# Three named double banks for scores and other products in a two-layer attention kernel

## The chip, the cores and the metric

The kernel runs on one core of one Trainium2 chip. The metric is the device time of one launch in microseconds (us), the median of three runs: 4044.44 us before the change (4041.61 to 4047.32). TensorE is called PE here, VectorE DVE, ScalarE ACT, GpSimd POOL and SyncE SP, as in the profile. [...]

## The reference

The input x is 4 images of 32 x 32 tokens with 768 channels, float32. Two layers run one after the other, each with a residual:

```
x = x + L0(gn(x))      # q, k, v = h @ W + b;  softmax(q k / 8 + bias_h + bias_w) v;  @ Wp + bp
x = x + L1(gn(x))      # the same, but each of q, k, v goes through a depthwise 3x3
                       # convolution and a layer norm over each head's 64 channels,
                       # and q is added to the head's output before the projection
```

`gn` is a group norm over 32 groups. There are 12 heads of 64 channels. The position bias of a query and a key is the query times a table that depends on the distance of their rows, plus the same for their columns. All is in float32.

## The kernel before, in words

The eight stages are images in pairs: images 0 and 1 in layer 0, the same two in layer 1, then images 2 and 3. A stage has six items, one for each pair of heads (two heads fill 128 partitions), so there are 48 items. An item's attention (`attend`) has 16 steps: two halves of the queries (512 columns), and in each two groups of four key tiles of 128 keys.

In a group, four chunks of scores come first. A chunk is a product of k and q for both heads (L669), to which a product of a one-hot matrix with the position bias is added (L671); ACT then takes its exponential (L676) out of two PSUM banks, one for each head. Behind the four chunks stands other work of PE, then the weighted sum of v for the four key tiles (L690, "av"), then other work again. DVE adds the exponentials up for the denominators (L682, L684).

The other work belongs to the next item: q, k and v products and what follows them. A table of steps (`plan`, `at`, `events`) says at which step each piece is issued; steps 0, 1, 4, 5, 8, 9, 12 and 13 fall behind scores and the others behind av. The order on PE, DVE, ACT and POOL is exactly the order of issue in the program (a manual schedule), so an instruction that waits holds up all that was issued later on its engine. Waits are set by the framework from which tile an instruction reads and writes. The pieces are:

- `plain` and `plain_v`, for the first two items: a product of 24 or 96 matmul records, and its evacuation by ACT (L410, L411, L419, L400).
- `sevens`, in the other items of layer 0: q and k of an item, or v of two items, come together out of seven products of quarters. The first call makes m4 into one bank, m3 into another, adds m2 to the first and m5 to the second; the second call makes m1 and m7, and adds m6 to m1's bank. ACT copies m4 out (L335), DVE adds (L330, L361, L375), ACT evacuates (L410, L419, L373).
- `padded`, in layer 1: a product, copied by ACT with its bias into a padded image in two parts (L442). `taps` is the convolution on DVE (L457, L459). `centre` takes the mean off by a product (ln_c), ACT squares it (L472) and copies it (L473). `squares` and `norm` finish the layer norm, `back` transposes with PE (ln_t) and ACT evacuates.
- `positions`: the position bias, 64 small matmuls into one bank (rel), copied by ACT in two parts (L522, L523); `split` divides it into two addends and sends them by POOL's DMA queue.
- `sums` and `result`: the denominators (z, L639), ACT's copy, Ln and Exp (L646 to L649), DVE's Newton step and the product with the weighted sum (L654 to L661). They are in a list `rest`, from which `more()` takes one entry at each place behind scores and behind av.
- `project`: the output product (proj), to which DVE adds bias and residual (L723). For the first image a product of weights and v bias (pbias, L713) is added to the bias first, in both layers.
- `group_norm` (two tiny products) and `mix_tokens` (sums of token quarters, L234) for the next stage.

Of PSUM's eight banks, scores have four (`ps_s`, two tiles of two banks, in turn), av has one, and all other products take one of three single banks in turn (`ps_m`, handed out by `bank`).

```
ps_s = pool("ps_s", 2, space=PSUM)
ps_av = pool("ps_av", 1, space=PSUM)
ps_m = pool("ps_m", 3, space=PSUM)
```

Of the kernel before, what the change touches and what calls it, by code (L numbers as in the profile page):

```python
# [9 lines left out]
F32 = mybir.dt.float32  # L10
# [7 lines left out]
P = 128  # L18
# [3 lines left out]
C = 768  # L22
# [23 lines left out]
def two_layers(ctx: ExitStack, tc: tile.TileContext, keep, x_in, wqkv, wproj, rels, windows, vrow, small, const, onehot, picks, out):  # L46
# [25 lines left out]
    work = pool("work", 2)  # L72
    one = pool("one", 1)
    stat = pool("stat", 3)
    ps_s = pool("ps_s", 2, space=PSUM)
    ps_av = pool("ps_av", 1, space=PSUM)
    ps_m = pool("ps_m", 3, space=PSUM)

    def bank(name):
        return ps_m.tile([P, 512], F32, tag="bank", name=name)  # L80

    def halves(ps, a, b, start=True, stop=True, **kw):

# [153 lines left out]
    def group_norm(stage):  # L237

        xn = xns[stage]
        st = stat.tile([P, NC * 2, 6], F32, tag="bn", name="bn", bufs=1)  # L240
        for n in range(NC):
            for h in range(2):
                nc.vector.bn_stats(st[:, 2 * n + h, :], xn[:, n, h * HALF : (h + 1) * HALF])
            if n in (1, 3):
                yield
        mv = stat.tile([P, 2], F32, tag="mv", name="mv")
        nc.vector.bn_aggr(mv, st.rearrange("p a b -> p (a b)"))
        yield
        yield
        group = cst[:, GROUP : GROUP + P]  # L250
        ps = bank("gn_mean")
        nc.tensor.matmul(ps[:, 0:1], group, mv[:, 0:1], start=True, stop=True)
        mean = stat.tile([P, 1], F32, tag="gmean", name="gmean")
        nc.vector.tensor_copy(mean, ps[:, 0:1])
        d = stat.tile([P, 1], F32, tag="gd", name="gd")
        nc.vector.tensor_sub(d, mv[:, 0:1], mean)
        nc.vector.scalar_tensor_tensor(d, d, d, mv[:, 1:2], ALU.mult, ALU.add)
        yield
        yield
        ps = bank("gn_var")  # L260
        nc.tensor.matmul(ps[:, 0:1], group, d, start=True, stop=True)
        v = stat.tile([P, 1], F32, tag="gv", name="gv")
        nc.vector.tensor_scalar(v, ps[:, 0:1], EPS, None, ALU.add)
        yield
        r = rsqrt(v, 1, "gn")
        yield
        for n in range(NC):
            nc.vector.tensor_scalar(xn[:, n, :], xn[:, n, :], mean, r, ALU.subtract, ALU.mult)  # L268
            if n % 2:
                yield  # L270
# [7 lines left out]
    sk = fixed.tile([P, NSMALL], F32, tag="sk", name="sk")  # L278
    nc.vector.tensor_scalar(sk, sm, SCALE, None, ALU.mult)

    pbias = fixed.tile([P, 2, NC], F32, tag="pbias", name="pbias")

    ones = fixed.tile([P, T], F32R, tag="ones", name="ones")
    plain = one.tile([P, T], F32, tag="whole", name="plain")
# [8 lines left out]
    class Pair:  # L293
# [15 lines left out]
        def sevens(self, s, second):  # L309

            xn = xns[self.b, self.layer]
            x11, x12, x21, x22 = (xn[:, n : n + 3, h : h + HALF] for n in (0, 3) for h in (0, HALF))

            def m(ps, at, x, more=False):

                w = weights[self.i, s, at // 2][:, 3 * (at % 2) : 3 * (at % 2) + 3, :]  # L320
                for t in range(4 if s else 1):
                    for n in range(3):
                        flags = dict(start=not (t or n or more), stop=n == 2, skip_group_check=True)
                        if s:
                            tokens = slice(t * P, (t + 1) * P)
                            halves(ps[:, tokens], x[:, n, tokens], w[:, n, :], **flags)
                        else:
                            halves(ps, w[:, n, :], x[:, n, :], **flags)

            add = lambda to, x, y, op=ALU.add: nc.vector.tensor_tensor(to, x, y, op)  # L330
            u, w = terms
            if not second:
                self.banks = b1, b2 = bank("m4m2"), bank("m3m5")
                m(b1, 0, x21)
                nc.scalar.copy(u, b1)  # L335
                m(b2, 1, x12)
                used((self.i, s, 0))
                add(u, u, b2)
                m(b1, 2, x11, more=True)
                add(w, u, b1, ALU.subtract)  # L340
                self.put(s, 1, 0, b1)
                m(b2, 3, x22, more=True)
                used((self.i, s, 1))
                add(u, u, b2, ALU.subtract)
                self.put(s, 0, 1, b2)
            else:
                b3, b4 = bank("m1m6"), bank("m7")
                m(b3, 4, quarters[0])
                add(u, u, b3)
                m(b4, 5, quarters[2])  # L350
                used((self.i, s, 2))
                self.put(s, 0, 0, b4, u)
                m(b3, 6, quarters[1], more=True)
                used((self.i, s, 3))
                self.put(s, 1, 1, b3, w)
# [258 lines left out]
    def attend(pair, os):  # L614
# [12 lines left out]
        for c in range(T // QC):  # L627
# [6 lines left out]

            def sums(weighed, acc, c=c):

                z = bank("z")
                for j in range(2):
                    nc.tensor.matmul(  # L639
                        z[j * D : (j + 1) * D, :], cst[:, ONES : ONES + D], acc[:, j, :],  # L640
                        start=True, stop=True,
                    )
                at = 2 * (pair.i * (T // QC) + c)
                t = work.tile([P, QC], F32, tag="t", name="t", bufs=1)
                inv = work.tile([P, QC], F32, tag="inv", name="inv", bufs=1)
                nc.scalar.activation(t, z, AF.Copy, accum_out=seen[:, at : at + 1])  # L646

                nc.scalar.activation(inv, t, AF.Ln, bias=tiny)
                nc.scalar.activation(inv, inv, AF.Exp, scale=-1.0, accum_out=seen[:, at + 1 : at + 2])  # L649
                return weighed, t, inv  # L650

            def result(weighed, t, inv, cols=cols):

                nc.vector.scalar_tensor_tensor(t, t, -1.0, inv, ALU.mult, ALU.mult)  # L654
                nc.vector.scalar_tensor_tensor(inv, t, 2.0, inv, ALU.add, ALU.mult)

                if pair.layer:
                    nc.vector.tensor_tensor(inv, weighed, inv, ALU.mult)
                    nc.vector.scalar_tensor_tensor(q[:, cols], inv, col(LN + 4), q[:, cols], ALU.mult, ALU.add)
                else:  # L660
                    nc.vector.tensor_tensor(q[:, cols], weighed, inv, ALU.mult)  # L661

            for g in range(0, NKT, 4):
                es = []
                for kt in range(g, g + 4):
                    keys = slice(kt * P, (kt + 1) * P)
                    ps = ps_s.tile([P, 2, QC], F32, tag="s", name="s")
                    for j, rows in enumerate(heads):
                        nc.tensor.matmul(ps[:, j, :], k[rows, keys], q[rows, cols], start=True, stop=False)  # L669
                    for j, rows in enumerate(heads):  # L670
                        nc.tensor.matmul(  # L671
                            ps[:, j, :], ones[rows, keys], bias[c][rows, kt // 2, :],
                            start=False, stop=True,
                        )
                    e = work.tile([P, 2, QC], F32, tag="e", name="e", bufs=4)
                    nc.scalar.activation(e, ps, AF.Exp)  # L676
                    es.append(e)
                more()
                if g == 0:
                    av = ps_av.tile([P, QC], F32, tag="av", name="av")  # L680
# [6 lines left out]
                for t, e in enumerate(es):  # L687
                    kt = g + t
                    for j in range(2):
                        nc.tensor.matmul(  # L690
                            av[j * D : (j + 1) * D, :], pair.vt[:, kt, j * D : (j + 1) * D], e[:, j, :],
                            start=(kt == 0), stop=(kt == NKT - 1),
                        )
                more()
                if g + 4 == NKT:
                    rest.extend((sums, result))
                    found = (copy(av), acc)
                yield
                yield
# [1 line left out]
    def project(stage, os):  # L701
# [3 lines left out]
        for m in range(NC):  # L705
            w = wp.tile([P, NC, P], F32, tag="wproj", name="wproj_t")
            nc.sync.dma_start(w, wproj[layer, :, :, m, :].rearrange("h p q -> p h q"))
            bias = col(BIAS[layer] + 18 + m)
            if b == 0:
                ps = bank("pbias")  # L710
                for n in range(NC):
                    v_bias = col(LN + 5) if layer else col(BIAS[0] + 12 + n)
                    nc.tensor.matmul(ps[:, 0:1], w[:, n, :], v_bias, start=(n == 0), stop=(n == NC - 1))  # L713
                nc.vector.tensor_tensor(pbias[:, layer, m : m + 1], ps[:, 0:1], bias, ALU.add)
            bias = pbias[:, layer, m : m + 1]
            for h in range(2):
                cols = slice(h * HALF, (h + 1) * HALF)
                x = wp.tile([P, HALF], F32, tag="x", name="x")
# [16 lines left out]
    for k in range(1, len(stages)):  # L735
# [5 lines left out]
        if stages[k][1] == 0:  # L741
            mix = mix_tokens(stages[k])
            for r in range(5):
                at(first + 5 * n_steps + r - (0 if stages[k - 1][1] else 8), lambda mix=mix: next(mix, None))
        elif stages[k - 1][1] == 0:
            at(first + 4 * n_steps + 6, lambda: [nc.gpsimd.memset(pad, 0.0) for pad in pads])
    mix = mix_tokens(stages[0])
# [29 lines left out]
    def check():  # L777
# [2 lines left out]
        nc.vector.tensor_reduce(total, seen, AX.X, ALU.add)  # L780
        good = stat.tile([P, 1], F32, tag="good", name="good")
        nc.vector.tensor_scalar(good, total, LIMIT, None, ALU.is_lt)
        ps = bank("good")
        nc.tensor.matmul(ps[:1, :1], cst[:, ONES : ONES + 1], good, start=True, stop=True)
        bad = keep.tile([1, 1], mybir.dt.int32, tag="bad", name="bad")
        nc.vector.tensor_scalar(bad, ps[:1, :1], -1.0, 1.0 * P, ALU.mult, ALU.add)
# [297 lines left out]
```

## Time and profile before

| | before |
|---|---|
| median of 3 runs | 4044.44 us |
| profiled execution, its own time | 4040.44 us |
| its span, first to last instruction | 4038.7 us |
| mean granted TensorE clock | 0.996 |
| PE busy, share of the span | 3945.2 us, 98% |
| DVE busy | 2494.3 us, 62% |
| ACT busy | 1812.1 us, 45% |
| POOL busy | 409.8 us, 10% |

All times of the sections below come from this one execution, so sums are made against its 4040.44 us. A row of the groups reads: line, engine, operation, tile written and tiles read, shape, count, then busy us and mean ns of one, then the idle time of the engine just ahead of them and what ended most of it. In a timeline the first number is the start in us from the span's start and the second the length; rows that follow each other on an engine are merged. A wait's row has the us in total, the times, and the longest. "PEld" is PE loading weights, which overlaps with its products.

### The profile page before, as it was taken

The page shows a single profiled execution, that of the slowest core. Times are in us where ns is not written, and L with a number is a line of the kernel's source. Part 1 is how long each engine was busy: PE and PEld are TensorE (multiplying, and loading weights), DVE is VectorE, ACT ScalarE, POOL GpSimd, SP SyncE. Part 2 cuts the span into 40 slices and gives each one's busy share as a digit, 9 for nine tenths or more (in the row PEclk, how much of TensorE's full clock was granted, in tenths as well). Part 3 has the DMA queues.
Part 4 walks back from the last instruction along what each step waited for, and adds up shares of the span by engine and source line. Part 5 has one row for each costly group of instructions (what it writes and reads, how often), then busy time and mean ns, then how long its engine had stood idle before and what let it go on. Part 6 is the DMA issues. An engine that isn't in the chain of part 4 may idle for free.

```text
span 4038.7 us, 79929 instructions
## 1 busy us (share of the span) xinstructions
PE 3945.2 (98%) x35098; PEld 1720.3 (43%) x35098; DVE 2494.3 (62%) x2800; ACT 1812.1 (45%) x2669; POOL 409.8 (10%) x776
## 2 busy tenths in 40 slices
PE   7999999999999999999899999999999999999999
PEld 3534444434344444444444344354343444434443
DVE  2455423558489985799633454245575898848883
ACT  2444424545255553455423544244443555525552
POOL 0111100110000110010011110001100011000010
PEclk9999999999999999999999999999999999999999
DMA  5333242221411222212133222422114112131112
GB/s 160 85 112 113 71 128 73 57 65 38 132 48 38 76 52 75 63 49 69 41 103 88 58 70 63 144 58 70 47 53 127 37 43 53 40 104 43 38 47 75
DMA packets 179046, 293.34 MB, mean 73 GB/s; under 512 B 22528, under 2 KB 77952, under 8 KB 178688
## 3 DMA queue, kind: packets, MB, share of 16 engines
q1 hardware_dynamic: 117248, 187.41, 14.8%
q0 software_dynamic: 61440, 100.71, 10.9%
q8 instruction: 279, 4.57, 0.5%
q14 instruction: 79, 0.65, 0.1%
HBM read 153.36 MB, written 34.01 MB: 46 GB/s over the span
## 4 chain that ended last, share of the span: by engine, by line
PE 85%; DVE 8%; ACT 3%; issue 1%; DMA 1%; POOL 0%; DVEq 0%; SPq 0%; ACTq 0%
PE qkv L85 18%; PE av L690 14%; PE s L669 14%; PE proj L85 12%; PE m3m L85 4%; PE m4m L85 4%; PE m1m L85 4%; PE s L671 3%; PE ln_c L85 3%; PE rel L517 3%; PE z L639 2%; DVE shared L459 2%; DVE acc L684 2%; PE m L85 2%; ACT e L676 2%
## 5 line engine op out<-in xcount | busy, mean ns | idle before, releaser
L676 ACT ACTIVATE e<-s 128x1024 f32<-128x1024 f32 x768 | 781.3, 1023 | 529.8 <-PE s L671 503.7
L669 PE MATMUL s<-q,k 64*128 64x512 f32 x3072 | 831.8, 618 | 27.9 <-ACT e L676 22.2
L684 DVE TENSOR_TENSOR acc<-acc,e 128x1024 f32<-128x1024 f32 x576 | 705.4, 1225 | 184.4 <-ACT e L676 133.4
L85 PE MATMUL qkv<-xn,wqkv_t 128*64 128x512 f32 x3648 | 815.6, 596 | 2.8 <-DVE xn L268 2.6
L459 DVE SCALAR_TENSOR_TENSOR shared<-shared,sm 128x1056 f32<-128x1056 f32 x576 | 758.3, 1316 | 14.9
L671 PE MATMUL s<-bias,ones 64*128 64x512 f32 x1536 | 615.6, 794 | 13.9 <-DMA bias<-whole 9.5
L690 PE MATMUL av<-e,vt 128*64 128x512 f32 x2624 | 594.5, 595 | 0.0
L544 POOL DMA_DIRECT2D bias<-high x384 | 204.1, 552 | 3356.5 <-ACT high L533 3097.9
L85 PE MATMUL proj<-q,wproj_t 128*64 128x512 f32 x2304 | 504.9, 593 | 0.0
L85 PEld LDWEIGHTS qkv<-xn,wqkv_t 128*64 128x64 f32 x3648 | 252.9, 137 | 488.5 <-issue 482.6
L669 PEld LDWEIGHTS s<-q,k 64*128 64x128 f32 x3072 | 255.4, 186 | 362.0 <-ACT e L676 210.6
L442 ACT ACTIVATE shared<-qkv,sm 128x512 f32<-128x512 f32 (+1 forms) x288 | 129.2, 501 | 595.6 <-PE qkv L85 595.6
L723 DVE SCALAR_TENSOR_TENSOR x<-proj,pbias,x 128x512 f32<-128x512 f32 x96 | 72.1, 751 | 439.4 <-PE proj L85 435.0
L690 PEld LDWEIGHTS av<-e,vt 128*64 128x64 f32 x2624 | 184.7, 137 | 347.5 <-issue 328.9
L682 DVE TENSOR_TENSOR acc<-e 128x1024 f32<-128x1024 f32 x96 | 117.6, 1225 | 345.4 <-ACT e L676 344.6
L85 PEld LDWEIGHTS proj<-q,wproj_t 128*64 128x64 f32 x2304 | 163.7, 137 | 313.5 <-issue 311.7
L671 PEld LDWEIGHTS s<-bias,ones 64*128 64x128 f32 x1536 | 150.2, 188 | 199.6 <-issue 193.6
L544 POOL DMA_DIRECT2D bias<-whole x384 | 204.9, 562 | 119.5 <-DVE whole L534 109.0
L632 ACT COPY weighed<-av 128x512 f32<-128x512 f32 x96 | 56.3, 586 | 329.2 <-PE av L690 329.2
L85 PEld LDWEIGHTS ln_c<-cst,shared 128*64 128x64 f32 x2304 | 131.4, 138 | 44.4 <-issue 34.6
L517 PEld LDWEIGHTS rel<-q,rel 64*32 64x32 f32 x6144 | 111.6, 105 | 78.0 <-issue 61.0
L85 PE MATMUL ln_c<-cst,shared 128*64 128x128 f32 x2304 | 139.2, 274 | 3.1 <-DVE shared L459 3.1
(119 smaller groups left out, 3613.0 us busy)
## 6 DMA issues: line engine op xcount, KB each, us to landing
bias<-high POOLq DMA_DIRECT2D x384, 128.0 KB, 2.8
bias<-whole POOLq DMA_DIRECT2D x384, 128.0 KB, 3.0
wqkv_t<-in_wqkv SPq DMA_DIRECT2D x78, 384.0 KB, 3.1
wqkv_t<-mixed SPq DMA_DIRECT2D x66, 384.0 KB, 3.1
wproj_t<-in_wproj SPq DMA_DIRECT2D x48, 384.0 KB, 3.7
wqkv_t<-in_wqkv SPq DMA_DIRECT2D x66, 192.0 KB, 2.5
xn<-in_x SPq DMA_DIRECT2D x24, 512.0 KB, 7.8
x<-in_x SPq DMA_DIRECT2D x48, 256.0 KB, 2.8
```

The source lines that it names most:

```text
L85: nc.tensor.matmul(ps[lo : lo + D], a[:, lo : lo + D], b, start=start, stop=stop, **kw)
L442: nc.scalar.activation(self.pad[s][:, rows, there : there + src.shape[2]], src, AF.Identity, bias=col(self.column(s)))
L459: nc.vector.scalar_tensor_tensor(y, window, tap, y, ALU.mult, ALU.add)
L517: nc.tensor.matmul(ps[lo : lo + S, k * S : (k + 1) * S].rearrange("p (b c) -> p b c", b=2), rel[rows, 2 * self.layer + i, first : first + ...
L544: nc.gpsimd.dma_start(sets, some.unsqueeze(1).to_broadcast([D // 2, 2, QC]))
L639: nc.tensor.matmul(z[j * D : (j + 1) * D, :], cst[:, ONES : ONES + D], acc[:, j, :], start=True, stop=True,)
L669: nc.tensor.matmul(ps[:, j, :], k[rows, keys], q[rows, cols], start=True, stop=False)
L671: nc.tensor.matmul(ps[:, j, :], ones[rows, keys], bias[c][rows, kt // 2, :], start=False, stop=True,)
L676: nc.scalar.activation(e, ps, AF.Exp)
L682: nc.vector.tensor_tensor(acc, es[0], es[1], ALU.add)
L684: nc.vector.tensor_tensor(acc, acc, e, ALU.add)
L690: nc.tensor.matmul(av[j * D : (j + 1) * D, :], pair.vt[:, kt, j * D : (j + 1) * D], e[:, j, :], start=(kt == 0), stop=(kt == NKT - 1),)
```

## The change

`ps_s` and `ps_m` go. In their place are three named tiles of two banks each, A, B and C (`ps_two`), and one single bank (`ps_small`). The four chunks of scores of a group take A, B, C and A. Other products take halves of doubles: behind scores in the order B, C, A, behind av in the order C, B; `bank` takes a new double when no half is left, and every place starts with a new one. `sevens` takes its first two banks as the halves of C, m7 as a half of C and m1 with m6 in the single bank. z, the group norm's products, layer 1's pbias and the last check use the single bank as well.

Beside that, layer 0's v bias is no longer taken through the projection: `result` leaves the weighted mean in `inv`, and a third entry `finish` in `rest` writes q from it by an ACT activation with the bias (layer 0 only, 48 times). The pbias products of layer 0 (six) go. The five pieces of `mix_tokens` for the third image come at steps 0, 0, 0, 1, 1 of the item where they had steps 0 to 4.

```diff
-    ps_s = pool("ps_s", 2, space=PSUM)
+    ps_two = pool("ps_two", 1, space=PSUM)
     ps_av = pool("ps_av", 1, space=PSUM)
-    ps_m = pool("ps_m", 3, space=PSUM)
+    ps_small = pool("ps_small", 1, space=PSUM)
+    BEHIND_SCORES, BEHIND_AV = "BCA", "CB"
+    order, left = list(BEHIND_AV), []
+
+    def other_work(places):
+        order[:] = places
+        left.clear()
+
+    def banks(name, place=None):
+        if place is None:
+            place = order.pop(0)
+            order.append(place)
+            left.clear()
+        return ps_two.tile([P, 2, 512], F32, tag=place, name=name)

     def bank(name):
-        return ps_m.tile([P, 512], F32, tag="bank", name=name)
+        if not left:
+            two = banks(name)
+            left.extend((two[:, 0, :], two[:, 1, :]))
+        return left.pop(0)
+
+    def small_bank(name):
+        return ps_small.tile([P, 512], F32, tag="small", name=name)
...
             if not second:
-                self.banks = b1, b2 = bank("m4m2"), bank("m3m5")
+                two = banks("m4m2_m3m5", "C")
+                b1, b2 = two[:, 0, :], two[:, 1, :]
...
-                b3, b4 = bank("m1m6"), bank("m7")
+                b3, b4 = small_bank("m1m6"), banks("m7", "C")[:, 0, :]
...
-                z = bank("z")
+                z = small_bank("z")
...
-                    nc.vector.tensor_tensor(q[:, cols], weighed, inv, ALU.mult)
+                    nc.vector.tensor_tensor(inv, weighed, inv, ALU.mult)
+                return (inv,)
+
+            def finish(inv, cols=cols):
+                if not pair.layer:
+                    nc.scalar.activation(q[:, cols], inv, AF.Identity, bias=col(pair.column(2)))
...
-                for kt in range(g, g + 4):
+                for kt, place in zip(range(g, g + 4), "ABCA"):
                     keys = slice(kt * P, (kt + 1) * P)
-                    ps = ps_s.tile([P, 2, QC], F32, tag="s", name="s")
+                    ps = banks("s", place)
...
+                other_work(BEHIND_SCORES)
                 more()
...
+                other_work(BEHIND_AV)
                 more()
                 if g + 4 == NKT:
-                    rest.extend((sums, result))
+                    rest.extend((sums, result, finish))
...
-            if b == 0:
-                ps = bank("pbias")
-                for n in range(NC):
-                    v_bias = col(LN + 5) if layer else col(BIAS[0] + 12 + n)
...
+            if layer:
+                if b == 0:
+                    ps = small_bank("pbias")
...
-                at(first + 5 * n_steps + r - (0 if stages[k - 1][1] else 8), lambda mix=mix: next(mix, None))
+                at(first + 5 * n_steps + (r // 3 if stages[k - 1][1] else r - 8), lambda mix=mix: next(mix, None))
```

More of the change, by code (lines that the diff above doesn't have):

```diff
@@ L250, in group_norm @@
         group = cst[:, GROUP : GROUP + P]
-        ps = bank("gn_mean")
+        ps = small_bank("gn_mean")
         nc.tensor.matmul(ps[:, 0:1], group, mv[:, 0:1], start=True, stop=True)
@@ L259, in group_norm @@
         yield
-        ps = bank("gn_var")
+        ps = small_bank("gn_var")
         nc.tensor.matmul(ps[:, 0:1], group, d, start=True, stop=True)
@@ L279, in two_layers @@
     nc.vector.tensor_scalar(sk, sm, SCALE, None, ALU.mult)
-    pbias = fixed.tile([P, 2, NC], F32, tag="pbias", name="pbias")
+    pbias = fixed.tile([P, NC], F32, tag="pbias", name="pbias")
     ones = fixed.tile([P, T], F32R, tag="ones", name="ones")
@@ L708, in project @@
             bias = col(BIAS[layer] + 18 + m)
-            if b == 0:
-                ps = bank("pbias")
-                for n in range(NC):
-                    v_bias = col(LN + 5) if layer else col(BIAS[0] + 12 + n)
-                    nc.tensor.matmul(ps[:, 0:1], w[:, n, :], v_bias, start=(n == 0), stop=(n == NC - 1))
-                nc.vector.tensor_tensor(pbias[:, layer, m : m + 1], ps[:, 0:1], bias, ALU.add)
-            bias = pbias[:, layer, m : m + 1]
+            if layer:
+                if b == 0:
+                    ps = small_bank("pbias")
+                    for n in range(NC):
+                        nc.tensor.matmul(ps[:, 0:1], w[:, n, :], col(LN + 5), start=(n == 0), stop=(n == NC - 1))
+                    nc.vector.tensor_tensor(pbias[:, m : m + 1], ps[:, 0:1], bias, ALU.add)
+                bias = pbias[:, m : m + 1]
             for h in range(2):
@@ L782, in check @@
         nc.vector.tensor_scalar(good, total, LIMIT, None, ALU.is_lt)
-        ps = bank("good")
+        ps = small_bank("good")
         nc.tensor.matmul(ps[:1, :1], cst[:, ONES : ONES + 1], good, start=True, stop=True)
```

## The prediction

> **What bounds the kernel now.** I read the page's busy times first: TensorE (PE) is busy in 98% of the span.
>
> ```profile
> PE 3945.2 (98%) x35098; PEld 1720.3 (43%) x35098; DVE 2494.3 (62%) x2800; ACT 1812.1 (45%) x2669; POOL 409.8 (10%) x776
> ```
>
> So only two things shorten the span: less work on PE, or fewer of its 93 us of idle time. Anything that makes PE wait lengthens it one for one. Next come PE's own waits (total us, times, longest us).
>
> ```profile
> PE s L669 <- ACT e L676: 22.2, 43, 1.8
> ...
> PE s L671 <- DMA bias<-whole: 9.5, 4, 2.9
> ...
> PE ln_t L495 <- ACT shared L473: 1.8, 2, 0.9
> ```
>
> The largest repeated one is scores waiting for an exponential (L676) to empty a bank. Waits for the emptying of other products' banks hardly exist: two of 0.9 us. The timeline of one group of four score chunks shows the rest of what a chunk loses (start, length).
>
> ```profile
> 1013.59 1.13 PE L669 MATMUL s<-q,k 64*128 64x512 f32 x4
> ...
> 1014.78 1.03 PE L669 MATMUL s<-q,k 64*128 64x512 f32 x4
> 1014.98 2.11 ACT L676 ACTIVATE e<-s 128x1024 f32<-128x1024 f32 x2 [10.63 <-PE s L671]
> ...
> 1016.06 1.13 PE L669 MATMUL s<-q,k 64*128 64x512 f32 x4
> ```
>
> The second chunk starts 1.19 us after the first, the third 1.28 us after the second: it starts 0.02 us after the first exponential ends (1014.98 + half of 2.11). So the third chunk loses 0.09 us at best. Summed over the groups of the trace, against 1.19 us a chunk, the loss is 39 us: about 17 of it are 192 times 0.09, the rest are groups behind L517 (rel), where two copies delay ScalarE (third chunk at 1.63 us), and a few of 3 us.
>
> Then the timeline of a layer 0 product from quarters, because it shows how evacuations now run beside PE.
>
> ```profile
> 2497.63 2.74 PE L85 MATMUL m3m<-xn,wqkv_t 128*64 128x512 f32 x12
> 2497.85 0.59 ACT L335 COPY shared<-m4m 128x512 f32<-128x512 f32 x1 [0.38 <-PE m4m L85]
> 2500.20 2.74 PE L85 MATMUL m4m<-xn,wqkv_t 128*64 128x512 f32 x12
> 2500.49 0.69 DVE L330 TENSOR_TENSOR shared<-shared,m3m 128x512 f32<-128x512 f32 x1 [1.28 <-PE m3m L85]
> 2502.78 2.74 PE L85 MATMUL m3m<-xn,wqkv_t 128*64 128x512 f32 x12
> 2503.00 0.69 DVE L330 TENSOR_TENSOR shared<-shared,m4m 128x512 f32<-128x512 f32 x1 [1.82 <-PE m4m L85]
> 2503.72 0.69 ACT L419 ACTIVATE k<-m4m,sk 128x512 f32<-128x512 f32 x1 [5.29 <-DVE shared L330]
> ```
>
> Each product starts 2.57 us after the one before, and the copy out of its predecessor's bank runs under it.
>
> **What the changed program says.** A double bank is one tile, and in the program as built the first matmul into one half waits for the engine that reads the other half. The same four products, before and after, in the order of PE with the semaphores waited for:
>
> ```
> before  m4m2<-xn [waits DMAHW0,DVE]             m3m5<-xn [waits DMAHW1]
>         m4m2<-xn [waits DMAHW2,Activation]      m3m5<-xn [waits DVE]
> after   m4m2_m3m5<-xn [waits DMAHW0,DVE,Activation]  m4m2_m3m5<-xn [waits DMAHW1,Activation]
>         m4m2_m3m5<-xn [waits DMAHW2,DVE]             m4m2_m3m5<-xn [waits Activation]
> ```
>
> Followed to the value waited for, the second product (m3) waits for the copy of m4 (L335), the third (m2) for VectorE's sum with m3, the fourth (m5) for the k evacuation of m4+m2 (L419). In the timeline above these end at 2498.44, 2501.18 and 2504.41, that is 0.81, 0.98 and 1.63 us after PE had begun the product which would now wait. The same holds for every pair of halves handed out by `bank`: I count 300 products whose first matmul waits for the evacuation of the product directly ahead in the same double. Before, evacuations of the product directly ahead hold such a matmul in a handful of places.
>
> [...] L419 starts only when VectorE's L330 on that bank is done, which makes m5's wait the sum of both. [...] In windows of the trace (us, PE busy, ..., granted clock, DMA):
>
> ```profile
> 1960.00:1967.00 7.00, 1.48 (x12) 0.57 (x10) 6.86 (x8) 2.05 (x2) 0.00 (x0) 0.75 0.00 0
> 1967.00:1974.50 7.50, 7.50 (x28) 2.33 (x30) 6.79 (x6) 0.59 (x1) 0.00 (x0) 0.78 0.00 0
> ```
>
> PE idles 5.5 us there and its clock is 0.75 and 0.78 around it. Gaps of 1.8 us elsewhere show no such drop.
>
> **Costs, part by part.** A stall is the evacuation's length plus handoffs: 0.12 to 0.22 us from the start that PE would have had to the evacuation's start (2497.63 to 2497.85), 0.06 from its end to PE's start (ln_t at 1919.05 behind a copy ending 1918.99), and some 0.05 for weights not loaded ahead: 0.27 us. Durations are from the groups by shape; the long ones:
>
> ```profile
> L442 ACT ACTIVATE shared<-qkv,sm 128x512 f32<-128x512 f32 x144 | 100.0, 695 | 595.6 <-PE qkv L85 595.6
> L523 ACT COPY whole<-rel 64x512 f32<-64x512 f32 x96 | 99.7, 1039 | 1.1
> ...
> L522 ACT COPY whole<-rel 64x512 f32<-64x512 f32 x96 | 55.2, 575 | 126.3 <-PE rel L517 126.3
> ...
> L442 ACT ACTIVATE shared<-qkv,sm 128x32 f32<-128x32 f32 x144 | 44.4, 308 | 0.0
> ```
>
> - Quarters: 22 of q and k, 0.59 + 0.69 + (0.69 + 0.69) = 2.65 us each, 58 us; 11 of v, 2.55 each, 28 us (99 waits).
> - A product behind a padded layer 1 product in its double: 70 times 0.695 + 0.308, 70 us.
> - Behind rel: 32 times 0.575 + 1.039, 52 us.
> - Behind proj (L723, 0.751): 33 times, 25 us.
> - Second half of ln_t: 24 times k at 0.77, 6 times q and q_t at 0.77 + 1.28, 31 us.
> - Second half of ln_c behind Square and copy (L472, L473): 6 times 1.19, 7 us; plain layer 0 products, 6 times, 5 us.
>
> These are 276 waits and 276 us, plus 276 x 0.27 = 75. Then 24 ln_c halves that come behind z: ScalarE first does z's copy, Ln and Exp, and at 1914.7 to 1919 the copy ends at 1918.99 where PE would start the half at 1916.49: 2.5 us, 24 times, with handoff 62 us. Sum 413. Reading the delay of each of the 300 straight from where the evacuation ended in the trace gives 428, as in some places VectorE or ScalarE was late already; I take 420.
>
> - Scores: the second chunk needs B. Where rel's second half is the third product behind AV it sits in B: copies end 1.79 us after it, the chunk comes after 1.19, so 0.6 late, some 18 times; behind ln_c 0.1, 24 times: 12 us.
> - Clock: stalls of 2.5 us may cost part of a window of 3.4 us at half clock, 1.7 us each; not shown for such gaps, so 0 to 40 us, I take 10 (one in four of the 24).
> - Gains: the third chunk's wait goes, since its bank C was last used by products behind AV that end at least 2.4 us before, and the fourth waits for an exponential that ended over 1 us before: 37 of 39 us (the 3 us cases move half to the fourth). Layer 0's bias products: half of the 18.0 us of L713, 9 us. The earlier token sums at one stage border: at most PE's 5.5 us wait for L234, taken whole. Slack for DMA and VectorE: half of the 25 us that PE waits for bias loads and late vector work, 12 us. Gains 63.
> - At nothing: 48 activations of layer 0's v bias, about 0.7 us each on ScalarE (33 us), queued behind a group's exponentials and covered by AV (3.4 us); if uncovered, at most 33. VectorE's result writes another tile at the same 0.69. Bias loads on POOL's queue and weights on SP's keep their order; what is issued behind a late evacuation is late with PE.
>
> Sum: 420 + 12 + 10 - 63 = +379, on 4040.4 us of the profiled execution 4420; the median stands 4 us above it, so 4424.
>
> **Rivals.** *The waits are covered* (other side): if evacuations ended before PE gets to the second half, only gains remain, 4044 - 63 = 3981. It decides where a wait costs under 63/300 = 0.21 us; the shortest evacuation alone is 0.59 and starts only when PE ends the first half. For it: only that ScalarE is 45% busy. *Backlog counted twice*: waits let ScalarE and VectorE catch up, and z's chain or late sums hide under earlier stalls; 24 x 1.5 off ln_c, 0.15 less handoff on 276 and twice the slack is 36 + 41 + 12, so about 4335. Against: the three steps are in a fixed order with nothing else between. *The clock falls*: layer 1 pairs have six stalls of 1 to 2.5 us; with four half-clock windows in each of 24 pairs 24 x 4 x 1.7 = 163 us more, 4587. Against: 1.8 us gaps show no drop.
>
> **Numbers.** Forecast 0.80, backlog 0.09, clock 0.07, covered 0.03, something that cancels to no change 0.01. The forecast's own range is 4350 (handoff 0.15, no clock loss, more slack) to 4505 (handoff 0.4, clock 40). With a part of both neighbours, 4340 to 4515. 0.2% is about what this kernel's measurement can tell from no change: slower 0.96, same 0.01, faster 0.03.
>
> **What would show it.** PE's share falls to about 89% with some 470 us idle, busy time of its groups about equal; its waits name ACT at the padding activation (about 85 us), rel's copies (about 60), Square and copy of ln_c (about 70), VectorE's L330 and proj. The third chunk starts 1.19 us after the second. A plain layer 1 pair takes 86 us for 77. I am wrong if PE has no such waits, or if its clock falls well below 0.99.

## The result, and the profile after

The changed kernel takes 4398.89 us (median of 4 runs, 4394.53 to 4402.41), the kernel before 4043.03 us beside it: the ratio is 1.0878, with a 95% interval of 1.0859 to 1.0897. The forecast was 4424 us in a range of 4340 to 4515. The profiled execution took 4397.79 us, its span 4395.9 us.

The page's busy times after the change:

```profile
PE 3976.0 (90%) x35026; PEld 1722.2 (39%) x35026; DVE 2494.6 (57%) x2794; ACT 1849.2 (42%) x2717; POOL 411.5 (9%) x776
```

PE has 72 records fewer (the bias products of layer 0) and yet 31 us more busy time, and its idle time is 420 us where it was 93 (some 470 were forecast). PE's waits after the change (total us, times, longest):

```profile
PE ln_c L109 <- ACT shared L498: 65.8, 30, 2.4
PE rel L109 <- ACT whole L548: 55.9, 30, 2.6
PE qkv L109 <- ACT shared L467: 51.9, 52, 1.0
PE m4m_m3m L109 <- ACT k L444: 33.2, 22, 1.5
PE m4m_m3m L109 <- DVE shared L354: 33.0, 33, 3.1
PE proj L109 <- DVE x L756: 24.8, 29, 0.9
PE m4m_m3m L109 <- ACT shared L360: 22.5, 33, 0.7
PE ln_t L520 <- ACT k L444: 20.9, 24, 0.9
...
PE qkv L520 <- ACT shared L467: 18.0, 18, 1.0
```

A double's second product carries the name of its first in these rows ("qkv L520" is a transpose in the second half of a qkv double). The counts are those of products directly behind another in the same double: 33 groups of quarters, 30 times rel, 52 + 18 = 70 times behind a padded product. The wait for an exponential, the largest repeated wait before, no longer appears.

Four products of quarters of the same kind as in the timeline of before (an earlier item's):

```profile
2335.51 0.59 ACT L360 COPY shared<-m4m_m3m 128x512 f32<-128x512 f32 x1 [0.38 <-PE m4m_m3m L109]
2336.15 2.79 PE L109 MATMUL m4m_m3m<-xn,wqkv_t 128*64 128x512 f32 x12 [0.69 <-ACT shared L360]
2339.07 0.69 DVE L354 TENSOR_TENSOR shared<-shared,m4m_m3m 128x512 f32<-128x512 f32 x1 [2.17 <-PE m4m_m3m L109]
2339.81 2.80 PE L109 MATMUL m4m_m3m<-xn,wqkv_t 128*64 128x512 f32 x12 [0.86 <-DVE shared L354]
2342.65 0.69 DVE L354 TENSOR_TENSOR shared<-shared,m4m_m3m 128x512 f32<-128x512 f32 x1 [2.90 <-PE m4m_m3m L109]
2343.37 0.69 ACT L444 ACTIVATE k<-m4m_m3m,sk 128x512 f32<-128x512 f32 x1 [7.27 <-DVE shared L354]
2344.11 2.37 PE L109 MATMUL m4m_m3m<-xn,wqkv_t 128*64 128x512 f32 x10 [1.51 <-ACT k L444]
```

Each evacuation that ran under the next product now stands between two products. PE starts 0.05 us after each of them ends; the waits are 0.69, 0.86 and 1.51 us. The starts of such products, 2.57 us apart before, are 3.43 (2332.72 to 2336.15), 3.66 and 4.30 us apart.

The scores went the other way. One group in the timeline after the change:

```profile
1069.59 1.13 PE L700 MATMUL s<-q,k 64*128 64x512 f32 x4
...
1070.78 1.02 PE L700 MATMUL s<-q,k 64*128 64x512 f32 x4
1070.98 4.29 ACT L707 ACTIVATE e<-s 128x1024 f32<-128x1024 f32 x4 [11.71 <-PE s L702]
...
1071.87 1.02 PE L700 MATMUL s<-q,k 64*128 64x512 f32 x4
...
1072.95 1.02 PE L700 MATMUL s<-q,k 64*128 64x512 f32 x4
```

The second chunk still starts 1.19 us after the first, but the third and the fourth start 1.09 and 1.08 us after the one ahead (1.28 and 1.20 before).

With the same products of both traces paired, and each measured from its start to the start of the next, the 355 us between the first product and the last divide so:

| stretch | after less before |
|---|---|
| from a product to a tied product behind it in the same double | +420 us |
| first to second chunk of scores, 192 groups | +6 us |
| second to third chunk | -56 us |
| third to fourth chunk | -23 us |
| all other stretches (9 us of it in products behind a stall) | +8 us |

### The profile page after: what moved, and what is told of

It reads as the page before. It is cut to its first block, busy times and chain, and to the rows that moved or that the text cites. A ratio compares the mean times of both kernels' runs of the same rounds, so it can differ in the third digit from the quotient of the medians.

```text
span 4395.9 us, 80010 instructions
## 1 busy us (share of the span) xinstructions
PE 3976.0 (90%) x35026; PEld 1722.2 (39%) x35026; DVE 2494.6 (57%) x2794; ACT 1849.2 (42%) x2717; POOL 411.5 (9%) x776
## 4 chain that ended last, share of the span: by engine, by line
PE 82%; ACT 8%; DVE 6%; issue 1%; DMA 1%; POOL 0%; SPq 0%; DVEq 0%; ACTq 0%
PE qkv L109 17%; PE s L700 14%; PE av L722 14%; PE proj L109 10%; PE m4m_m3m L109 8%; PE rel L109 4%; PE s L702 4%; PE m1m L109 4%; PE rel L542 2%; PE ln_c L109 2%; PE m L109 2%; ACT shared L467 1%; PE z L664 1%; DVE acc L716 1%; ACT whole L548 1%
## 5 line engine op out<-in xcount | busy, mean ns | idle before, releaser
L109 PE MATMUL qkv<-xn,wqkv_t 128*64 128x512 f32 x3072 | 695.8, 603 | 4.1 <-DVE xn L292 2.3
L109 PE MATMUL proj<-q,wproj_t 128*64 128x512 f32 x1872 | 423.6, 604 | 24.8 <-DVE x L756 24.8
L700 PEld LDWEIGHTS s<-q,k 64*128 64x128 f32 x3072 | 276.5, 186 | 275.3 <-issue 204.1
L109 PEld LDWEIGHTS qkv<-xn,wqkv_t 128*64 128x64 f32 x3072 | 216.5, 139 | 427.0 <-issue 420.3
L467 ACT ACTIVATE shared<-qkv,sm 128x512 f32<-128x512 f32 x240 | 107.7, 502 | 547.4 <-PE qkv L109 547.4
L109 PE MATMUL m4m_m3m<-xn,wqkv_t 128*64 128x512 f32 x1056 | 247.6, 604 | 73.9 <-ACT k L444 33.2
L109 PEld LDWEIGHTS proj<-q,wproj_t 128*64 128x64 f32 x1872 | 132.2, 139 | 299.2 <-issue 248.6
L354 DVE TENSOR_TENSOR shared<-shared,m4m_m3m 128x512 f32<-128x512 f32 x99 | 68.0, 687 | 295.1 <-PE m4m_m3m L109 295.1
L109 PE MATMUL ln_c<-cst,shared 128*64 128x128 f32 x1632 | 112.6, 282 | 66.3 <-ACT shared L498 65.8
L109 PE MATMUL rel<-xn,wqkv_t 128*64 128x512 f32 x576 | 132.1, 608 | 43.0 <-ACT whole L548 43.0
```

The costliest lines, as they stand in the source:

```text
L109: nc.tensor.matmul(ps[lo : lo + D], a[:, lo : lo + D], b, start=start, stop=stop, **kw)
L467: nc.scalar.activation(self.pad[s][:, rows, there : there + src.shape[2]], src, AF.Identity, bias=col(self.column(s)))
```

## The experiments

My theory was that nearly the whole loss is the tie between the halves of one double. The rival was that places are too few: scores and other products now share doubles, and wait for what lay there last.

**One product for a double.** `bank` and `sevens` of the changed kernel are edited so that no two other products lie in one tile:

```diff
-        if not left:
-            two = banks(name)
-            left.extend((two[:, 0, :], two[:, 1, :]))
-        return left.pop(0)
+        return banks(name)[:, 0, :]
...
-                two = banks("m4m2_m3m5", "C")
-                b1, b2 = two[:, 0, :], two[:, 1, :]
+                left.clear()
+                b1, b2 = banks("m4m2", "C")[:, 0, :], banks("m3m5", "B")[:, 0, :]
```

> The changed kernel, but a double gives only its first bank to a product, so that no two other products lie in one tile (m4 with m2 in C, m3 with m5 in B). Theory: nearly all of the loss is the wait of a second half for the evacuation of the first. The time from the start of one product to the start of the next grew by 420 us at these places against before; they go, and the gains on scores, the v bias and the token sums stay: 3970 to 4000 us, below the kernel before. Rival, too few places: scores and other products now share B and C, and a product waits for what lay there; with one product for a double there are half as many places, so it stays at 4390 us or gets longer.

Measured: 3982.41 us, 0.9852 of before (0.9835 to 0.9868). With half as many places the loss is gone, and the kernel is 61 us faster than the one before. The longest of PE's waits in it:

```profile
PE gn_mean L273 <- DVE mv L268: 16.4, 1, 16.4
PE qkv L106 <- ACT k L441: 9.5, 22, 0.4
PE s L699 <- DMA bias<-whole: 9.5, 5, 2.4
```

The first is the start of the kernel, which the kernel before has too. The quarters stand 2.57 us apart again in its timeline of PE:

```profile
2454.48 2.75 PE L106 MATMUL m3m<-xn,wqkv_t 128*64 128x512 f32 x12
2457.05 2.75 PE L106 MATMUL m4m<-xn,wqkv_t 128*64 128x512 f32 x12
2459.63 2.75 PE L106 MATMUL m3m<-xn,wqkv_t 128*64 128x512 f32 x12
```

So sharing doubles with scores costs next to nothing (all waits of scores for ScalarE come to 5 us in this trace, 23 us before); the rival falls.

**Only the quarters apart.** In the changed kernel the second of the two edits alone:

> The changed kernel, only the first two banks of the products of quarters are halves of two doubles (C and B) in place of the two halves of C. Theory: the three waits in each of the 33 groups of quarter products go, which took 118 us of the 420: about 4280 us. Rival, too few places: no change or longer, as B is taken up as well.

Measured: 4271.71 us, ratio 1.0563 (1.0545 to 1.0581), 127 us less than the changed kernel against 118 forecast. All other tied waits stay as they were (ln_c 65.8 us, rel 55.9, behind padded products 51.9 and 18.0).

**Halves in turn.** The changed kernel's `bank` gives the first half of one double, then the first half of the next, then the second halves; quarters in C and B.

```diff
...
+        if len(left) == 2:
+            ready.append(True)
+        if ready:
+            half = left.pop(0)
+            if not left:
+                ready.clear()
+            return half
+        place = order.pop(0)
+        order.append(place)
+        two = ps_two.tile([P, 2, 512], F32, tag=place, name=name)
+        left.append(two[:, 1, :])
+        return two[:, 0, :]
...
```

> The changed kernel with all its places, two products to a double, but the halves are given out in turn: first half of one double, first half of the next, then their second halves (quarter products in C and B). Theory: the evacuation of a first half runs under the product between, so nearly all of the 420 us go; 22 products behind the two halves of ln_c still meet the late copy of ln_c, about 1.5 us each: 4005 to 4035 us. Rival, too few places: as many places as in the changed kernel, so about 4398 us.

Measured: 4035.04 us, 0.9979 of before (0.9972 to 0.9986): the upper end of what was expected. Of the changed kernel's 4399 us, 364 go. Some 127 of them are the quarters, which here share no tile, as in the experiment above. In the rest two products still share a tile, but another product now lies between the two. What is left of the ties shows in its waits:

```profile
PE ln_c L118 <- ACT shared L507: 32.3, 22, 1.5
```

These are the 22 products behind ln_c that were foretold at 1.5 us. Two smaller waits of the layer norm's products come to 10 us. PE's granted clock was at half for 10 us more than in the first experiment; half of such time is lost (matmul pairs start 0.85 us apart in it, 0.43 behind it), 5 us; the last section has these windows. So 47 of the 59 us between the two profiled executions are named; 53 us lie between the medians.

**Scores in A, B, A, B.** The first experiment's kernel, with two doubles for scores:

```diff
-    BEHIND_SCORES, BEHIND_AV = "BCA", "CB"
+    BEHIND_SCORES, BEHIND_AV = "CAB", "CB"
...
-                for kt, place in zip(range(g, g + 4), "ABCA"):
+                for kt, place in zip(range(g, g + 4), "ABAB"):
```

> As the kernel with one product for a double, but scores take A, B, A, B (other products behind scores C, A, B). It measures what the third double is worth to scores alone. The third and fourth chunk start 1.087 us after the one before in the changed kernel, and took 1.28 and 1.20 us before, summed 79 us: if that is the third double's, this kernel is 70 to 85 us longer than the one with A, B, C, A. If only the wait that I saw in the third chunk was its cost (0.09 us and the late groups), it is 37 to 40 us longer.

Measured: 4086.18 us, ratio 1.0108 (1.0092 to 1.0125), 104 us more than with A, B, C, A and so outside both expectations. Two waits in it, the first of which the edit brought along, since with this order rel stands in C just ahead of the v quarters:

```profile
PE m4m L106 <- ACT whole L545: 27.9, 11, 2.6
PE s L697 <- ACT e L704: 20.5, 41, 1.4
```

Between the two profiles, the stretches from each chunk's start to the next start took 912 us with three doubles and 982 with two. So the third double is worth 70 us to scores. The accident in C is 28 us, and 24 us more at half clock are worth 12. That makes 110 us where the profiles differ by 105, so some 5 us of it were gained elsewhere or are counted twice. The upper reading, not the one of my prediction, holds.

**The small parts alone,** on the kernel before: v bias by ScalarE, then the token sums.

```diff
-                    nc.vector.tensor_tensor(q[:, cols], weighed, inv, ALU.mult)
+                    nc.vector.tensor_tensor(inv, weighed, inv, ALU.mult)
+                return (inv,)
...
-                    rest.extend((sums, result))
+                    rest.extend((sums, result, finish))
```

> The kernel before with one part of the change alone: layer 0's v bias by an activation of ScalarE behind the product with the denominators, and no bias products in layer 0. Forecast: the six bias products go, 9 us, and the 48 activations are hidden under the weighted sum: 4034 us, 0.9978 of before. If they are not hidden, up to 33 us come on top: up to 4067 us.

Measured: 4031.85 us, 0.9974 of before (0.9965 to 0.9984), a gain of 12 us. The 48 activations at 0.71 us are covered.

```diff
-... + r - (0 if stages[k - 1][1] else 8), ...
+... + (r // 3 if stages[k - 1][1] else r - 8), ...
```

> The kernel before with the token sums of the third image at steps 0, 0, 0, 1, 1 in place of 0 to 4, alone. Forecast: at most the 5.5 us that PE waits at one stage border for the last of them: 4038 us, 0.9986 of before. If the vector work that they pass then comes late instead, no change.

Measured: 4040.16 us, 0.9994 (0.9985 to 1.0002). No change can be told from this; a gain of 5.5 us is inside the interval, and so is none.

**The tie alone, in the kernel before.** Its scores and their banks stay; two of the three single banks become halves of one tile:

```diff
-    ps_m = pool("ps_m", 3, space=PSUM)
+    ps_m = pool("ps_m", 1, space=PSUM)
+    turn = []
...
-        return ps_m.tile([P, 512], F32, tag="bank", name=name)
+        if len(turn) == 2:
+            turn.clear()
+            return ps_m.tile([P, 512], F32, tag="bank", name=name)
+        if turn:
+            turn.append(None)
+            return turn[0][:, 1, :]
+        turn.append(ps_m.tile([P, 2, 512], F32, tag="two", name=name))
+        return turn[0][:, 0, :]
```

> The kernel before, scores in their own two doubles as ever, v bias and token sums as before; only two of the three single banks of the other products are now the halves of one tile of two banks, given out in the same turn (first half, second half, single bank). It puts in the suspected cause alone, without sharing any bank between scores and products. Theory: the first matmul of a second half waits for the evacuation of the first. Read from where these evacuations ended in the trace of before, 253 products wait 292 us, less where one wait has already covered the next: 4290 to 4360 us. Rival, the loss comes of scores and products sharing doubles: no change, 4043 us.

Measured: 4362.57 us, ratio 1.0793 (1.0775 to 1.0811). The same memory, the same turn and the same work, but one tile in place of two, and most of the changed kernel's loss is there. PE's longest kinds of wait:

```profile
PE ln_c L93 <- ACT shared L481: 59.1, 33, 2.4
PE rel L93 <- ACT whole L531: 28.4, 15, 2.6
PE s L677 <- ACT e L684: 20.0, 43, 1.4
```

It is 2.6 us above what I expected; PE's clock was at half for 99 us of this span, against 27 us before, which I had left out.

**One kind of tie in the fastest kernel.** The first experiment's kernel, with ln_c's two halves in one double:

```diff
+            two = banks("ln_c")
             for h in range(2):
                 cols = slice(h * HALF, (h + 1) * HALF)
-                ps = bank("ln_c")
+                ps = two[:, h, :]
```

> The kernel with one product for a double, but the two halves of ln_c lie in one double, 72 times. It puts one kind of tie alone into the fastest kernel. Theory: 24 stalls of about 2.5 us (k, behind z) and 48 of about 1.4 us, 127 us, so 4109 us, and if the stalls of over 2 us are what halves PE's clock for windows of 3.4 us (some 15 more in the changed kernel than before), about 25 us more: 4134 us, and as many such windows as in the changed kernel. If the clock windows come of something else: 4109 us.

Measured: 4102.42 us, ratio 1.0145 (1.0128 to 1.0162), 120 us above the kernel without the tie.

```profile
PE ln_c L106 <- ACT shared L496: 113.5, 72, 2.4
```

All 72 waits are there, and the time is 7 us below the lower of the two expectations: the waits came to 113.5 us where 127 were foretold. Clock windows at half speed rise from 7 to 12, not to 22: five of them come behind its 24 stalls of 2.1 to 2.4 us, and no more. The last section says which five.

## Why the prediction was right, point by point

**PE as the bound** held: PE's idle time and the span grew by 326 and 357 us, and the 31 us between them are busy time, to which time at half clock adds. The products behind a stall are longer in the rows (2.79 for 2.74 us, 0.05 more, as much as the forecast's estimate for weights not loaded ahead), and they no longer begin within the modelled end of the one ahead.

**The ties.** I put 420 us on 300 waits, and the stretches that hold them grew by 420 us. That agreement is partly luck: 36 us of half clock more than before fall into these stretches, worth 18 us, and four of the six removed bias products (1.43 us from start to start) lay in them. So the ties themselves are nearer 408 us. By kind, the visible waits were close to what I named: padded products 70 us (forecast about 85, with handoffs that are not recorded as idle), rel's copies 59 (60), ln_c 66 (70). That they are the cause is shown from both sides: untied, the loss goes; tied in the kernel before, it comes.

**The second chunk's wait for B** was given as 12 us; the stretch from first to second chunk grew by 6 us, and PE's recorded wait is 7.4 us behind rel's copies, 18 times 0.4.

**The clock** was priced at 10 us and cost about 26: the changed kernel spent 78.5 us of its span at half clock and the one before 27.3, and half of the difference is lost. The window of 3.4 us behind the price is in the trace of before: where PE idles for 5.5 us, the granted clock is 1.00 from 1960.0 to 1963.4, 0.51 to 1966.8, 0.50 to 1970.2 and 0.99 to 1973.6. The step that failed is "one in four of the 24": nine windows followed stalls of ln_c where six were reckoned, and nine more followed the stalls of 2.0 us and more behind rel and q_t, which had been left out. "Not shown for such gaps" was a misreading as well: in the trace of before, PE's gap of 2.26 us that ends at 1935.40 is followed by such a window (granted clock 0.51 from 1936.1 to 1939.5).

**The gain on scores** was the term most wrong: 37 us in the sum, 79 us in the trace (56 + 23). I took 1.19 us as a chunk's own length and called everything over it loss. In truth the next chunk can start after 1.09 us. In the loads of weights (PEld) one can see what made the difference. Before, second and third chunk of a group:

```profile
1014.55 0.42 PEld L669 LDWEIGHTS s<-q,k 64*128 64x128 f32 x4 [0.23 <-issue]
...
1016.06 0.30 PEld L669 LDWEIGHTS s<-q,k 64*128 64x128 f32 x4 [0.65 <-ACT e L676]
```

The second chunk's loads begin 0.23 us ahead of its products (1014.78). The third's wait with them for the exponential, and begin when they do (1016.06); the chunk behind it starts 1.20 us later in place of 1.09. With three doubles the third chunk's loads are ahead again, here in the kernel with one product for a double:

```profile
991.16 0.42 PEld L697 LDWEIGHTS s<-q,k 64*128 64x128 f32 x4 [0.24 <-issue]
991.39 1.02 PE L697 MATMUL s<-q,k 64*128 64x512 f32 x4
```

So a late bank costs its wait and, as well, some 0.1 us for loads that could not run ahead. That the third double is what brings this is shown by A, B, A, B, which lost 70 us; that it is the loads was only read from the timelines, no run separates it.

**Small parts.** The v bias gained 12 us alone (9 forecast), with the cover named (AV). The token sums could not be told from nothing. The 12 us of slack were not measured apart: PE's waits for bias loads fell from 14 to 6.6 us.

**The sum.** Forecast +379 us, measured +357 in the profile. Against the sum, ties and B came to some 18 us less, the clock to 16 us more and scores to 42 us less; the token sums and the slack, 17 us of gain in the forecast, are not to be seen outside the scores (the rest of the stretches grew by 8 us in all). The errors have both signs and mostly cancel. A layer 1 pair took 85.3 us where it took 76.9, against 86 forecast.

**The rivals.** "The waits are covered" asked for less than 0.21 us a wait; the shortest kind measured 0.68. "Backlog counted twice" would have shown in shorter stalls late in a chain, but m5 behind m2 waited 1.51 us, as the fixed order said. "The clock falls" went the right way by 26 of its 163 us.

## What to carry to other kernels

Bank names and places were sound here: three doubles in turn for scores are worth 70 us, and products may share them. What cost 9% was that two independent products lay in one tile, and in these programs waits are set by tile: two of the three single banks before, as one tile, made the time 1.0793 of what it was. Where an allocation puts several buffers into one tile, follow the waits of the built program through one turn before the order is tuned: a first matmul that waits for the reader of the product just ahead leaves nothing to run under that reader.

## What the runs showed of the hardware that I had not expected

- In these traces a chunk's weight loads wait for the same exponential as its products. A chunk whose loads ran ahead is followed by the next after 1.09 us, one whose loads didn't after 1.19 or 1.20 us. So the third chunk that seemed 0.09 us late before cost 0.30 us in its group: 0.19 of waiting (1.28 less 1.09) and 0.11 behind it (1.20 less 1.09). That the loads are the reason is a reading of the timelines.
- PE idle stretches of 2.0 to 3.0 us can be followed by a window of 3.4 us at half clock. In the changed kernel, around the ln_c stall that ends at 1078.47 (us, PE busy, ..., granted clock, DMA):

```profile
1075.50:1078.40 2.90, 0.59 (x12) 0.35 (x8) 2.69 (x3) 2.84 (x7) 0.00 (x0) 1.00 0.79 257
1078.80:1082.20 3.40, 3.40 (x21) 1.85 (x18) 2.42 (x3) 1.07 (x2) 0.00 (x0) 0.51 0.00 0
1082.20:1085.60 3.40, 3.40 (x18) 1.15 (x16) 0.00 (x0) 0.00 (x0) 0.00 (x0) 0.99 0.00 0
```

The clock is at half for the 3.4 us that follow the stall of 2.38 us, and full again then. In the window the pairs of matmul records of qkv start 0.85 us apart, behind it 0.43, so half of a window is lost. 2.38 us without PE were enough here. There are 7 windows in the kernel before, 22 in the changed one, 7 with one product for a double (some of them two steps long).

Which stalls cost a window can be read from the traces. Within each of the ten, the windows begin whole steps of 3.413 us apart, to 0.003 us. Cut the span into these steps, its first 31 and last 12 us left out, and add up PE's idle time in each step that is at full clock itself. In the ten traces together 113 such steps had 2.00 us of idle time or more, and a window followed every one (6 of them are in the kernel before). Of the 22 windows in the changed kernel, 21 come behind such a step; below 2.00 us a window is rare (22 steps in the ten traces). So in these traces the place of a stall counts as well as its length. Of the 24 stalls in the last experiment, the five that were followed by a window put 2.31 to 2.38 us into one step; the others were divided by a border, and no step around them holds more than 1.93 us. No run moved a stall on purpose to test this.
